# Layer 1's latent attention: two of four probability rows transposed by VectorE and DMA instead of TensorE

## The chip, the core and the metric

The kernel runs on one core of one Trainium2 chip. The core has TensorE for matrix products (PE in the profile, its weight loads PEld), VectorE (DVE), ScalarE (ACT), GpSimd (POOL) and SyncE (SP), which issues most of the DMAs; 16 DMA engines carry them. The metric is the time of one execution on the device in microseconds, given as the median of several runs.

## What is computed

The reference is a four-layer model on 2,048 tokens of width 256 in float32. Each layer adds an attention-like part and a feed-forward part to its input; both read the same layer norm. The change lies in layer 1's attention, a latent attention with 16 heads and 4 sequences of 512 tokens:

```
scores = einsum('bqhd,bkhd->bhqk', qf, kf) * softmax_scale
causal = tril(ones((s, s)))
scores = where(causal, scores, min)
attn   = softmax(scores, axis=-1)
out    = einsum('bhqk,bkhd->bqhd', attn, v)
return out.reshape(b, s, N_HEADS * D_V) @ wo
```

Layer 1's feed-forward part is a product-key lookup (for each token the best 8 of 512 experts, whose rows are gathered from DRAM) and a gated MLP.

## The kernel before

Everything is float32. Streams of work are written as Python generators, and `weave` takes steps from several of them in turn, by costs that each step yields. Layer 1 (`layer1`) weaves four: the latent attention (`latent_pieces`), the product-key lookup (`product_key_pieces`), the rest of the gated MLP (`glu_pieces`), and at the end the routing of layer 2. The scheduler then orders each engine's instructions by its own priorities, except where the kernel pins them (`tc.keep_in_program_order`, or `c.chain`, which ties each pinned instruction to the last pinned one).

The attention works on the latent form: keys of 64 latent and 64 rotary dimensions are shared by all heads (`kf`), values are the 64 latent dimensions (`cv`), and the value and output projections are multiplied together ahead (`wz`, by `carry`). The loop over `s` runs through 64 head-sequences (16 heads times 4 sequences). Two successive `s`, an even and an odd one, are a pair `p` that shares one query projection, one value product and one output projection's half.

For each `s` there are four rows of 128 queries, row `i` having `(i+1)*128` keys (causal):

- `probabilities(s, i)`: a score matmul on PE (L985), an eviction on DVE that adds the mask and finds the row's extreme (L988, writes `pr` and `nm`), an exponential on ACT that also sums (L992), a reciprocal on DVE (L1108) and a scaling by it on ACT (L1110). Buffers `pr0` to `pr3` are double.
- `turned(s-1, j)`: the value product needs the probabilities with the keys on the partitions. PE transposes each 128x128 block (L1117), 10 blocks per `s`, into PSUM tiles `tr`; DVE (for j = 0 and 2) or ACT (for j = 1 and 3) copies them into `PT` (L1121). This is done one `s` behind the scores.
- `queries(p+1)`, in every even `s`: matmuls (L1072 to L1077), an ACT copy to `pes`, four DMAs on SP that swap its quarters into `psw` (L1082), two ACT scalings into `qf`. `rotate`, in the next odd `s`, applies the rotary tables on DVE (L1091 to L1094) and completes `qf`.
- the value product of pair p (L1253): 8 matmuls of 512, 384, 256 and 128 columns, the two heads in the two column halves of the array (64 output columns each), then an ACT copy to `zT` (L1259). After every second pair, the output projection (L1267) and its addition to `x` on DVE (L183).

`product_key_pieces` first ranks experts (8 rounds, each with a DMA `routed<-both` and back on SP, L1359 and L1361), then for each of 16 token tiles loads `tok` by SP (L1369), gathers 8 experts on GpSimd's queue (L1371), multiplies on DVE (L1381) and adds on DVE (L177).

Layer 3's attention (`full_attention`), which the change does not touch, already transposes on DVE and DMA: DVE transposes within 32x32 blocks (L1598, tile `Y`), four DMAs write the strips of 32 partitions to a DRAM buffer (L1603), one DMA on the same queue reads it back in the wanted order (L1607, `PT`), and the value product (L1642) reads `PT` in blocks of 128 columns made of four runs of 32.

Of the kernel before, what the change touches and what calls it, by code (L numbers as in the profile page):

```python
# [16 lines left out]
P = 128  # L17
# [3 lines left out]
TPB = SEQ // P  # L21
# [9 lines left out]
class Ctx:  # L31


    def __init__(self, tc, stack):
        self.tc, self.nc = tc, tc.nc
        self.stack = stack
        self.n = 0
        pool = lambda name, **kw: stack.enter_context(tc.tile_pool(name=name, **kw))
        self.keep = pool("keep", bufs=1)
        self.ln = pool("ln", bufs=1)  # L40
        self.psum = pool("psum", bufs=4, space=bass.MemoryType.PSUM)
        self.users, self.then, self.later, self.pinned = {}, None, [], False
        self.trickle, self.chained = [], None

    def tile(self, pool, shape, tag, dtype=F32, **kw):
        self.n += 1
# [11 lines left out]
    def chain(self, ins):  # L58


        last, self.chained = self.chained, ins.ins
        if last is not None:
            self.tc.add_manual_dep(
                ins.ins, last.name,
                mybir.DependencyInfo(mybir.DependencyClass.NoSync, mybir.DependencyReason.DATA),
                reason="chain",
            )
        return ins
# [942 lines left out]

def latent_pieces(c, a, keep, open_pool):

# [47 lines left out]
    def queries(p):  # L1063

        g, b, pair = p // 8, p // 2 % 4, p % 2
        if p % 8 == 0:
            carry(g)
        wpe0, wpe1, wl0, wl1, _ = weights[g]
        tokens = slice(b * SEQ, (b + 1) * SEQ)
        cols = slice(pair * P, (pair + 1) * P)  # L1070
        pe, pl = c.ps(), c.ps()
        nc.tensor.matmul(pl, lhsT=wl0[:, cols], rhs=qa0[:, tokens], start=True, stop=False)  # L1072
        upper = nc.tensor.matmul(pe, lhsT=wpe1[:, cols], rhs=qa1[:KL, tokens], start=True, stop=False)
        with tc.issue_after(upper.ins), tc.high_priority(offset=200):
            nc.tensor.matmul(pl, lhsT=wl1[KL:, cols], rhs=qa1[KL:, tokens], start=False, stop=True)
        with tc.high_priority(offset=100):
            nc.tensor.matmul(pe, lhsT=wpe0[:, cols], rhs=qa0[:, tokens], start=False, stop=True)  # L1077

        pes, psw = (c.tile(pool, [P, SEQ], n, bufs=1) for n in ("pes", "psw"))
        nc.scalar.copy(pes, pe)  # L1080
        for to in range(0, P, 32):
            nc.sync.dma_start(psw[to : to + 32, :], pes[to ^ 32 : (to ^ 32) + 32, :])  # L1082
        qf = c.tile(pool, [P, 2, SEQ], "qf")
        nc.scalar.mul(qf[:KL, 0, :], pl[:KL, :], -scale)
        nc.scalar.mul(qf[KL:, 1, :], pl[KL:, :], -scale)
        qfs[p] = qf
        return pes, psw, qf

    def rotate(pes, psw, qf):
        pec = c.tile(pool, [P, SEQ], "pec", bufs=1)  # L1090
        nc.vector.tensor_mul(pec, pes, cosq)  # L1091
        tc.keep_in_program_order(nc.vector.tensor_mul(psw, psw, sinq))
        nc.vector.tensor_add(qf[:KL, 1, :], pec[:KL, :], psw[:KL, :])
        nc.vector.tensor_add(qf[KL:, 0, :], pec[KL:, :], psw[KL:, :])  # L1094

    def probabilities(s, i):
        p, h = s // 2, s % 2
        b = p // 2 % 4
        if i == 0:
            totals[s] = c.tile(pool, [P, TPB], "total")  # L1100
        rinv = totals[s]
        prs[s].append(exp_scores(
            c, pool, late, qfs[p][:, h, :], kf[:, h, b * SEQ : (b + 1) * SEQ], i, rinv[:, i : i + 1]
        ))
        if i >= TPB - 2:

            done = slice(0, i + 1) if i < TPB - 1 else slice(i, i + 1)
            nc.vector.reciprocal(rinv[:, done], rinv[:, done])  # L1108
            for j in range(TPB)[done]:
                nc.scalar.mul(prs[s][j], prs[s][j], rinv[:, j : j + 1])  # L1110

    def turned(s, j):

        pt = c.ps("tr")
        n = SEQ - j * P
        for i in range(j, TPB):
            nc.tensor.transpose(  # L1117
                pt[:, (i - j) * P : (i - j + 1) * P], prs[s][i][:, j * P : (j + 1) * P], c.ident
            )
        copy = nc.scalar.copy if j % 2 else nc.vector.tensor_copy  # L1120
        return lambda: copy(PTs[s][:, START[j] : START[j] + n], pt[:, :n])  # L1121

    START = (0, 512, 896, 1152)
    qfs, prs, totals, PTs, zTs = {}, {}, {}, {}, {}
    rope = c.tile(pool, [P, SEQ], "psw", bufs=1)
    nc.scalar.dma_start(rope, a["l_rope"])
# [2 lines left out]
    def latents(b):  # L1129

        if b < 2:
            rooms = [c.tile(pool, [P, 1280], "PT")[:, :1024]]
        elif b == 2:
            rooms = [c.tile(pool, [P, SEQ], "zT", bufs=3) for _ in range(2)]
# [38 lines left out]
    for b in range(NB):  # L1173
        tokens = slice(b * SEQ, (b + 1) * SEQ)
        lats.append(latents(b))
        for t in range(TPB):
            tt = b * TPB + t
            pl = c.ps()[:, : QL + KL]
            project_tokens(c, pl, wa, slice(0, QL + KL), slice(tt * P, (tt + 1) * P))
            lat = lats[b][t]  # L1180
            nc.vector.tensor_copy(lat, pl)
            sq = c.tile(pool, [P, QL + KL], "pr1")
# [12 lines left out]
        rot = c.tile(pool, [P, SEQ], "pr3")  # L1195
        nc.vector.tensor_mul(rot, pk, rope)
        rots.append((rot, tokens))
        yield 1.2
# [16 lines left out]
        finish(b)  # L1215
        yield 1.9

    copy = None
    yield 1.9
    for s in range(65):  # L1220
        if s < 64:
            prs[s] = []
        for i in range(TPB):
            if s < 64:
                probabilities(s, i)
            if s > 0:
                if i == 0:
                    PTs[s - 1] = c.tile(pool, [P, 1280], "PT")
                ready, copy = copy, turned(s - 1, i)
                if ready:  # L1230
                    ready()
            if i == 0 and s % 2 == 1 and s < 63:
                rotate(*turning)
            yield 0.85
            if i == 1 and s % 2 == 0 and s < 62:
                turning = queries(s // 2 + 1)
                yield 2.6
        if copy:
            copy()
            copy = None  # L1240
        if s > 0:
            del prs[s - 1]
        if s % 2 == 1:
            continue
        if s == 0:
            continue

        p = s // 2 - 1
        g, b, pair = p // 8, p // 2 % 4, p % 2
        z = c.ps("acc")  # L1250
        for j in range(TPB):
            for h in range(2):
                tc.keep_in_program_order(nc.tensor.matmul(  # L1253
                    z[h * KL : (h + 1) * KL, j * P :], lhsT=cv[:, b * TPB + j, :],
                    rhs=PTs[s - 2 + h][:, START[j] : START[j] + SEQ - j * P],
                    start=(j == 0), stop=(j == TPB - 1),
                ))
        zTs[pair] = c.tile(pool, [P, SEQ], "zT", bufs=3)
        nc.scalar.mul(zTs[pair], z, kv_w)  # L1259
        yield 2.1  # L1260
        if pair == 1:
            wz = weights[g][4]
            for t in range(0, TPB, 2):
                po = v3(c.ps("acc"), DM)
                for j in range(2):
                    for k in range(2):
                        nc.tensor.matmul(  # L1267
                            po[:, j, :], lhsT=zTs[k][:, (t + j) * P : (t + j + 1) * P],
                            rhs=wz[:, k, :], start=(k == 0), stop=(k == 1),
                        )  # L1270
                add_pair(c, b * TPB + t, po)
                if g == 3 and t == TPB - 2:
                    c.part_done(b)
                yield 1.7


def product_key_pieces(c, a, keep, pool, dram, xn):
# [88 lines left out]
    def gather(t, k):  # L1366
        if k == 0:
            tok[t] = c.tile(pool, [P, DM], "tok", bufs=2)
            nc.sync.dma_start(tok[t], xn[t * P : (t + 1) * P, :])  # L1369
        e = c.tile(pool, [P, 2 * DM], "e", bufs=8)  # L1370
        nc.gpsimd.indirect_dma_start(  # L1371
            out=e, out_offset=None, in_=a["p_experts"],
# [36 lines left out]
def layer1(c, a, xn, following):  # L1409


    with ExitStack() as stack, ExitStack() as right:
# [7 lines left out]
        latent = latent_pieces(c, a, keep, lambda: pool_of("l_h", 2))  # L1420

        def glu_units():
            same = dict(tanh=True, bufs=5)
# [995 lines left out]
```

## Time and profile before

| What | Value |
|---|---|
| Median of 3 runs | 3007.26 us (3001.71 to 3009.33) |
| Profiled execution: own time | 2998.64 us |
| Profiled execution: span, mean granted clock | 2996.9 us, 0.988 |
| Busy: PE, DVE, ACT, POOL | 2892.5, 2136.6, 1391.8, 856.3 us |
| Scores of layer 1's attention, from the first 512-column score matmul to the last | 859 to 1470 us |

A group row reads: line, engine, operation, out<-in by the program's names, shape, count | busy us, mean ns of one | idle time of the engine just before, and what ended it. A float32 matmul is recorded as two passes, so counts of matmuls in the profile are twice the program's (transposes have one). Durations of matmuls overlap: what one costs in a row of many is the distance from one start to the next. "`<- issue`" marks time in which the engine waited for nothing that the profile shows.

### The profile page before, as it was taken

How to read it: one execution, taken by the hardware profiler on the slowest of the kernel's cores; microseconds unless marked ns; L12 is line 12 of the kernel's file. 1: busy time of each engine (PE TensorE's matmuls, PEld its weight loads, DVE VectorE, ACT ScalarE, POOL GpSimd, SP SyncE). 2: the span in 40 equal slices, each digit the busy share in tenths (PEclk: the TensorE clock that was granted, in tenths of full speed). 3: DMA queues.
4: the chain of work that ended last, by engine and by line, in shares of the span. 5: the costliest groups of instructions: out<-in, count | busy, mean ns of one | idle time of the engine just before them, and what ended most of it. 6: DMA issues, size and time to landing. Idle time of an engine off the chain costs nothing.

```text
span 2996.9 us, 40558 instructions
## 1 busy us (share of the span) xinstructions
PE 2892.5 (97%) x13812; PEld 1958.9 (65%) x13812; DVE 2136.6 (71%) x5434; ACT 1391.8 (46%) x3336; POOL 856.3 (29%) x681
## 2 busy tenths in 40 slices
PE   8999999999999999999978899999999999999999
PEld 5566666566755655555656588888888856666666
DVE  5777778787777787868643777777777756666666
ACT  4444445444376666656622454445444333333332
POOL 0565565656310033332023200000000033333331
PEclk9999999999999999999988999999999999999999
DMA  3333333242221145342223434443544300000000
GB/s 133 97 109 116 102 95 110 90 134 73 100 70 37 46 120 123 104 99 82 84 79 116 136 115 123 129 148 119 151 123 148 124 0 22 22 22 22 22 1 29
DMA packets 138366, 268.03 MB, mean 89 GB/s; under 512 B 19664, under 2 KB 99040, under 8 KB 133808
## 3 DMA queue, kind: packets, MB, share of 16 engines
q1 hardware_dynamic: 123696, 217.65, 23.1%
q0 software_dynamic: 14176, 47.01, 6.2%
q8 instruction: 109, 1.79, 0.2%
q14 instruction: 97, 0.79, 0.1%
q10 hardware_dynamic: 288, 0.79, 0.1%
HBM read 202.21 MB, written 54.26 MB: 86 GB/s over the span
## 4 chain that ended last, share of the span: by engine, by line
PE 81%; DVE 8%; ACT 4%; another core or an unknown queue 2%; issue 2%; POOL 1%; DMA 1%; SPq 0%; ACTq 0%; DVEq 0%; POOLq 0%
PE mm L329 16%; PE mm L159 14%; PE mm L985 7%; PE acc L329 6%; PE tr L329 6%; PE acc L1642 5%; PE acc L1001 4%; PE tr L823 3%; PE acc L1253 2%; PE tr L237 2%; PE acc L1267 2%; PE tr L1117 2%; PE acc L801 2%; PE mm L167 2%
## 5 line engine op out<-in xcount | busy, mean ns | idle before, releaser
L992 ACT ACTIVATE pr<-pr,nm 128x128 f32<-128x128 f32 (+3 forms) x512 | 286.1, 559 | 290.6 <-DVE nm L988 272.3
L988 DVE CUSTOM_DVE_ANT_0 pr<-mm,late 128x128 f32<-128x128 f32 (+3 forms) x512 | 245.6, 483 | 124.0 <-PE mm L985 108.1
L159 PE MATMUL mm<-xnT,wu 128*128 128x512 f32 x624 | 287.8, 599 | 0.0
L340 ACT COPY part<-mm 128x512 f32<-128x512 f32 (+1 forms) x372 | 177.7, 478 | 213.3 <-PE mm L329 205.0
L329 PE MATMUL mm<-token_sums,unit_sums 128*128 128x512 f32 (+1 forms) x624 | 267.5, 511 | 2.2 <-ACT part L340 2.2
L1371 POOL DMA_INDIRECT e<-in_p_experts,ids x128 | 130.0, 1016 | 477.1 <-DVE x L177 330.7
L159 PE MATMUL mm<-xnT,w_in 128*128 128x512 f32 x512 | 229.2, 593 | 0.6 <-DVE cy L591 0.6
L491 DVE SCALAR_TENSOR_TENSOR x<-acc,cw,x 128x128 f32<-128x128 f32 x372 | 128.8, 346 | 107.8 <-PE acc L329 106.1
L591 DVE SCALAR_TENSOR_TENSOR cy<-mm,ws,cy 128x509 f32<-128x509 f32 (+2 forms) x216 | 160.2, 744 | 51.1 <-ACT cy L587 47.2
L159 PEld LDWEIGHTS mm<-xnT,wu 128*128 128x128 f32 x624 | 115.4, 192 | 118.7 <-issue 110.9
L985 PE MATMUL mm<-kf,qf 128*128 128x128 f32 (+3 forms) x512 | 173.9, 442 | 3.1 <-DVE qf L1094 2.8
L985 PE MATMUL mm<-k,q 128*128 128x128 f32 (+3 forms) x512 | 172.0, 440 | 4.0 <-DVE nm L988 3.4
L761 POOL TENSOR_TENSOR G<-G,CB 128x1024 f32<-128x1024 f32 x64 | 151.5, 2367 | 81.7 <-DVE G L724 75.6
L744 ACT ACTIVATE xD<-xc,ws 128x128 f32<-128x128 f32 x256 | 83.9, 390 | 193.1 <-POOL y L785 183.6
L329 PEld LDWEIGHTS acc<-down_sums,hidden_sums 128*128 128x128 f32 x744 | 112.1, 192 | 85.1 <-issue 82.9
L159 PEld LDWEIGHTS mm<-xnT,w_in 128*128 128x128 f32 x512 | 96.5, 190 | 104.4 <-issue 94.9
L1642 PEld LDWEIGHTS acc<-PT,V 128*128 128x128 f32 x1280 | 154.5, 193 | 5.4 <-issue 2.0
L273 POOL TENSOR_TENSOR down_sums<-wu 128x256 f32<-128x256 f32 x8 | 5.9, 734 | 520.7 <-PE mm L329 411.9
L1642 PE MATMUL acc<-PT,V 128*128 128x128 f32 x1280 | 154.6, 276 | 0.0
L724 DVE TENSOR_TENSOR_SCAN G<-G,eye 128x1024 f32<-128x1024 f32 x64 | 148.2, 2315 | 0.0
L1117 PEld LDWEIGHTS tr<-con,pr 128*128 128x128 f32 x640 | 80.0, 142 | 92.0 <-issue 22.7
L474 DVE TENSOR_TENSOR whole<-mm,part 128x512 f32<-128x512 f32 x128 | 88.5, 692 | 68.4 <-PE mm L329 68.4
(440 smaller groups left out, 6783.6 us busy)
## 6 DMA issues: line engine op xcount, KB each, us to landing
turned<-Y SPq DMA_DIRECT2D x252, 160.0 KB
PT<-turned SPq DMA_DIRECT2D x63, 640.0 KB
G<-own SPq DMA_DIRECT2D x64, 512.0 KB
w_in<-in_m_units SPq DMA_DIRECT2D x16, 1024.0 KB
eb<-since SPq DMA_DIRECT2D x96, 128.0 KB
wu<-in_o_units SPq DMA_DIRECT2D x6, 1536.0 KB
wo<-in_m_units SPq DMA_DIRECT2D x16, 512.0 KB
psw<-pes SPq DMA_DIRECT2D x128, 64.0 KB
```

Source lines behind the costliest of these rows:

```text
L159: c.nc.tensor.matmul(out, lhsT=w[:, d, cols], rhs=c.xnT[:, d, tokens], start=(d == 0), stop=(d == 1))
L329: self.kept(self.c.nc.tensor.matmul(bank, lhsT=lhsT, rhs=rhs, start=first, stop=True, skip_group_check=not first))
L340: self.c.nc.scalar.copy(r, bank)
L591: nc.vector.scalar_tensor_tensor(y[:, j:], src[:, : SEQ - j], conv[:, k, 3 - j : 4 - j], y[:, j:], ALU.mult, ALU.add,)
L724: tc.keep_in_program_order(nc.vector.tensor_tensor_scan(flat, flat, eye.rearrange("p h t -> p (h t)"), 0.0, ALU.mult, ALU.add))
L761: nc.gpsimd.tensor_mul(G, G, seqs[b][2][:, t, :][:, None, :].to_broadcast([P, HG, P]))
L985: kept(nc.tensor.matmul(sc, lhsT=q[:, i * P : n], rhs=k[:, :n], start=True, stop=True))
L988: nc.vector.tensor_tensor_reduce(out=pr, in0=sc, in1=late[:, SEQ - n :], scale=scale, scalar=-NEG, op0=ALU.add, op1=ALU.min, accum_out=nm,)
L992: nc.scalar.activation(pr, pr, AF.Exp, bias=nm, scale=-1.0, accum_out=total)
L1117: nc.tensor.transpose(pt[:, (i - j) * P : (i - j + 1) * P], prs[s][i][:, j * P : (j + 1) * P], c.ident)
L1371: nc.gpsimd.indirect_dma_start(out=e, out_offset=None, in_=a["p_experts"], in_offset=bass.IndirectOffsetOnAxis(ap=ids[:, t, k : k + 1], ax ...
L1642: kept(nc.tensor.matmul(zs[:, i], lhsT=head["V"][:, j, h, :], rhs=head["PT"][:, :, i * (i + 1) // 2 + j, :], start=(j == 0), stop=(j == i),))
```

## The change

In layer 1's attention, rows 0 and 1 of each `s` (3 of the 10 blocks) are still transposed on PE, now in one PSUM tile with one ACT copy. Rows 2 and 3 (7 blocks) are transposed by DVE within 32x32 blocks into `Y`, written to DRAM by four DMAs on SP and read into `PT` by a fifth on SP, as in layer 3; the last `s` does them on PE. `PT` gets three buffers instead of two, `pr0` to `pr3`, `Y`, `pes` and `psw` have one, `zT` two. The value product becomes 20 matmuls of 128 columns and comes later: for the pair (2p, 2p+1) it stands in `s = 2p+3` after its third score. Score, transposition, query, value and output matmuls are chained in program order on PE, and the swap and strip DMAs in program order on SP (`chain` now keeps one chain per engine). One of the query projection's PSUM tiles moves from `mm` to `tr`. Reciprocals and scalings are done for rows 0 and 1 together and 2 and 3 together. `rotate` works in place. The `tok` loads of the product-key lookup move from SP's queue to GpSimd's. The gated MLP's and the lookup's own work is unchanged.

```diff
     def chain(self, ins):
-        last, self.chained = self.chained, ins.ins
+        last = self.chained.get(ins.ins.engine)
+        self.chained[ins.ins.engine] = ins.ins
...
-        pe, pl = c.ps(), c.ps()
...
+        pe, pl = c.ps(), c.ps("tr")
+        for out, lhsT, rhs, start, stop in (
+            (pl, wl0[:, cols], qa0[:, tokens], True, False),
+            (pe, wpe1[:, cols], qa1[:KL, tokens], True, False),
+            (pl, wl1[KL:, cols], qa1[KL:, tokens], False, True),
+            (pe, wpe0[:, cols], qa0[:, tokens], False, True),
+        ):
+            c.chain(nc.tensor.matmul(out, lhsT=lhsT, rhs=rhs, start=start, stop=stop))
...
-            nc.sync.dma_start(psw[to : to + 32, :], pes[to ^ 32 : (to ^ 32) + 32, :])
+            c.chain(nc.sync.dma_start(psw[to : to + 32, :], pes[to ^ 32 : (to ^ 32) + 32, :]))
...
-            c, pool, late, qfs[p][:, h, :], kf[:, h, b * SEQ : (b + 1) * SEQ], i, rinv[:, i : i + 1]
+            c, pool, late, qfs[p][:, h, :], kf[:, h, b * SEQ : (b + 1) * SEQ], i, rinv[:, i : i + 1],
+            kept=c.chain, bufs=1,
         ))
-        if i >= TPB - 2:
-            done = slice(0, i + 1) if i < TPB - 1 else slice(i, i + 1)
+        if i % 2:
+            done = slice(i - 1, i + 1)
...
-    def turned(s, j):
-        pt = c.ps("tr")
-        n = SEQ - j * P
-        for i in range(j, TPB):
-            nc.tensor.transpose(
-                pt[:, (i - j) * P : (i - j + 1) * P], prs[s][i][:, j * P : (j + 1) * P], c.ident
-            )
-        copy = nc.scalar.copy if j % 2 else nc.vector.tensor_copy
-        return lambda: copy(PTs[s][:, START[j] : START[j] + n], pt[:, :n])
+    def turn_strips(s, i):
+        if i == 2:
+            Ys[s] = c.tile(pool, [P, 896], "Y", bufs=1)
+        nc.vector.transpose(wide(Ys[s], i), strips(prs[s][i]))
+        if i == TPB - 1:
+            room = c.tile(dram, [4, 32, 4, 224], "strips")
+            PTs[s] = c.tile(pool, [P, 1280], "PT", bufs=3)
+            Y = Ys.pop(s)
+            for a in range(4):
+                c.chain(nc.sync.dma_start(
+                    room[:, :, a, :].rearrange("b r e -> r b e"),
+                    Y[a * 32 : (a + 1) * 32].rearrange("p (b e) -> p b e", b=4),
+                ))
+            c.chain(nc.sync.dma_start(PTs[s][:, :896], room.rearrange("b r a e -> (b r) (a e)")))
+
+    def turned(s, rows):
+        if s not in PTs:
+            PTs[s] = c.tile(pool, [P, 1280], "PT", bufs=3)
+        pt, n = c.ps("tr"), 0
+        for i in rows:
+            for j in range(i + 1):
+                c.chain(nc.tensor.transpose(
+                    pt[:, n * P : (n + 1) * P], prs[s][i][:, j * P : (j + 1) * P], c.ident
+                ))
+                n += 1
+        if rows[0] == 0:
+            return lambda: nc.scalar.copy(PTs[s][:, 896:], pt[:, : 3 * P])
+        return lambda: nc.scalar.copy(wide(PTs[s], rows[0]), strips(pt[:, : n * P]))
...
+    def values(p):
+        g, b, pair = p // 8, p // 2 % 4, p % 2
+        z = c.ps("acc")
+        for i in range(TPB):
+            for j in range(i + 1):
+                for h in range(2):
+                    c.chain(nc.tensor.matmul(
+                        z[h * KL : (h + 1) * KL, i * P : (i + 1) * P], lhsT=cv[:, b * TPB + j, :],
+                        rhs=block(2 * p + h, i, j), start=(j == 0), stop=(j == i),
+                    ))
...
-    for s in range(65):
+    for s in range(66):
...
+            if i == 0:
+                if s % 2 == 1 and s < 63:
+                    rotate(*turning)
+                yield from islice(pieces, 1)
+            if i == 1 and s % 2 == 0:
+                yield from islice(pieces, 1)
+                if s < 62:
+                    turning = queries(s // 2 + 1)
+                    yield 2.6
+            if i == 2 and s % 2 == 1 and s > 2:
+                pieces = values(s // 2 - 1)
+                yield 2.6
+            if i == TPB - 1 and s < 63:
+                turn_strips(s, 2)
+                turn_strips(s, 3)
+            if s < 64 and i == TPB - 1:
+                copy = turned(s, (0, 1))
...
-            nc.sync.dma_start(tok[t], xn[t * P : (t + 1) * P, :])
+            nc.gpsimd.dma_start(tok[t], xn[t * P : (t + 1) * P, :])
```

More of the change, by code (lines that the diff above doesn't have):

```diff
@@ L42, in __init__ @@
         self.users, self.then, self.later, self.pinned = {}, None, [], False
-        self.trickle, self.chained = [], None
+        self.trickle, self.chained = [], {}
     def tile(self, pool, shape, tag, dtype=F32, **kw):
@@ L1008, in heads_out, with latent_pieces @@
         yield 1.7
-def latent_pieces(c, a, keep, open_pool):
+def latent_pieces(c, a, keep, open_pool, dram):
     nc, tc = c.nc, c.tc
@@ L1070, in queries @@
         cols = slice(pair * P, (pair + 1) * P)
-        pe, pl = c.ps(), c.ps()
[L1072 to L1077, printed above, removed]
+        pe, pl = c.ps(), c.ps("tr")
[6 more added lines that the diff above has]
+            c.chain(nc.tensor.matmul(out, lhsT=lhsT, rhs=rhs, start=start, stop=stop))
         pes, psw = (c.tile(pool, [P, SEQ], n, bufs=1) for n in ("pes", "psw"))
@@ L1089, in rotate @@
     def rotate(pes, psw, qf):
-        pec = c.tile(pool, [P, SEQ], "pec", bufs=1)
-        nc.vector.tensor_mul(pec, pes, cosq)
+        nc.vector.tensor_mul(pes, pes, cosq)
         tc.keep_in_program_order(nc.vector.tensor_mul(psw, psw, sinq))
-        nc.vector.tensor_add(qf[:KL, 1, :], pec[:KL, :], psw[:KL, :])
-        nc.vector.tensor_add(qf[KL:, 0, :], pec[KL:, :], psw[KL:, :])
+        nc.vector.tensor_add(qf[:KL, 1, :], pes[:KL, :], psw[:KL, :])
+        nc.vector.tensor_add(qf[KL:, 0, :], pes[KL:, :], psw[KL:, :])
     def probabilities(s, i):
@@ L1110, in probabilities, with strips, wide, block @@
                 nc.scalar.mul(prs[s][j], prs[s][j], rinv[:, j : j + 1])
-    def turned(s, j):
-        pt = c.ps("tr")
-        n = SEQ - j * P
-        for i in range(j, TPB):
-            nc.tensor.transpose(
-                pt[:, (i - j) * P : (i - j + 1) * P], prs[s][i][:, j * P : (j + 1) * P], c.ident
-            )
-        copy = nc.scalar.copy if j % 2 else nc.vector.tensor_copy
-        return lambda: copy(PTs[s][:, START[j] : START[j] + n], pt[:, :n])
-    START = (0, 512, 896, 1152)
+    def strips(ap):
+        return ap.rearrange("p (j a s) -> p j a s", a=4, s=32)
+    def wide(tile, i):
+        lo = 0 if i == 2 else 3
+        return tile[:, :896].rearrange("p (a j s) -> p j a s", j=7, s=32)[:, lo : lo + i + 1]
+    def turn_strips(s, i):
[25 more added lines that the diff above has]
+        return lambda: nc.scalar.copy(wide(PTs[s], rows[0]), strips(pt[:, : n * P]))
+    def block(s, i, j):
+        if i < 2:
+            lo = 896 + (i + j) * P
+            return PTs[s][:, lo : lo + P]
+        return wide(PTs[s], i)[:, j]
+    Ys = {}
     qfs, prs, totals, PTs, zTs = {}, {}, {}, {}, {}
@@ L1131, in latents @@
         if b < 2:
-            rooms = [c.tile(pool, [P, 1280], "PT")[:, :1024]]
+            rooms = [c.tile(pool, [P, 1280], "PT", bufs=3)[:, :1024]]
         elif b == 2:
-            rooms = [c.tile(pool, [P, SEQ], "zT", bufs=3) for _ in range(2)]
+            rooms = [c.tile(pool, [P, SEQ], "zT", bufs=2) for _ in range(2)]
         else:
@@ L1181, in latent_pieces @@
             nc.vector.tensor_copy(lat, pl)
-            sq = c.tile(pool, [P, QL + KL], "pr1")
+            sq = c.tile(pool, [P, QL + KL], "pr1", bufs=1)
             nc.scalar.activation(
@@ L1194, in latent_pieces @@
         project(c, pk, wa, slice(256, 384), tokens)
-        rot = c.tile(pool, [P, SEQ], "pr3")
+        rot = c.tile(pool, [P, 896], "Y", bufs=1)[:, :SEQ]
         nc.vector.tensor_mul(rot, pk, rope)
@@ L1216, in latent_pieces, with out_pieces @@
         yield 1.9
-    copy = None
+    def values(p):
[8 more added lines that the diff above has]
+                    ))
+        for h in range(2):
+            del PTs[2 * p + h]
+        zTs[pair] = c.tile(pool, [P, SEQ], "zT", bufs=2)
+        nc.scalar.mul(zTs[pair], z, kv_w)
+        return out_pieces(g, b) if pair == 1 else iter(())
+    def out_pieces(g, b):
+        wz = weights[g][4]
+        for t in range(0, TPB, 2):
+            po = v3(c.ps("acc"), DM)
+            for j in range(2):
+                for k in range(2):
+                    c.chain(nc.tensor.matmul(
+                        po[:, j, :], lhsT=zTs[k][:, (t + j) * P : (t + j + 1) * P],
+                        rhs=wz[:, k, :], start=(k == 0), stop=(k == 1),
+                    ))
+            add_pair(c, b * TPB + t, po)
+            if g == 3 and t == TPB - 2:
+                c.part_done(b)
+            yield 1.7
+    copy, pieces = None, iter(())
     yield 1.9
-    for s in range(65):
+    for s in range(66):
         if s < 64:
@@ L1225, in latent_pieces @@
                 probabilities(s, i)
[L1226 to L1236, printed above, removed]
-                yield 2.6
-        if copy:
-            copy()
-            copy = None
@@ L1241, in latent_pieces @@
-        if s > 0:
-            del prs[s - 1]
[L1243 to L1274, printed above, removed]
+                yield 0.3
@@ new lines, in latent_pieces @@
+            if copy:
+                copy()
+                copy = None
+            if i == 0:
[9 more added lines that the diff above has]
+                pieces = values(s // 2 - 1)
+                yield 2.6
@@ L1277, in product_key_pieces @@
+            if i == TPB - 1 and s < 63:
[3 more added lines that the diff above has]
+                copy = turned(s, (0, 1))
+            if s == 64 and i < 2:
+                copy = turned(63, (i + 2,))
+            yield 0.5
+        if 0 < s < 64:
+            del prs[s - 1]
+    yield from pieces
 def product_key_pieces(c, a, keep, pool, dram, xn):
@@ L1419, in layer1 @@
         keep = pool_of("l_keep", 1)
-        latent = latent_pieces(c, a, keep, lambda: pool_of("l_h", 2))
+        strips = pool_of("l_dram", 2, space=bass.MemoryType.DRAM)
+        latent = latent_pieces(c, a, keep, lambda: pool_of("l_h", 2), strips)
         def glu_units():
```

## The prediction

> **What bounds the kernel now.** I read the page's first section, then engine busy times cut to layer 1's attention (859 to 1470 us) beside layer 3's (1710 to 2380 us), then the chain of waits and the groups by line in the first stretch.
>
> ```profile
> 859.00:1470.00 611.00, 582.99 (x2624) 341.83 (x2623) 477.56 (x1667) 398.58 (x1058) 122.96 (x122) 0.99 0.32 86
> 1710.00:2380.00 670.00, 660.92 (x3519) 554.79 (x3518) 503.88 (x1678) 327.05 (x927) 25.71 (x26) 0.99 0.45 133
> ```
>
> The columns are us, then busy us of PE, PEld, DVE, ACT and POOL, granted clock, DMA share, GB/s. PE is the busiest in both, DVE second at 78%. Busy PE contains drained pipelines, so I count spacings instead: passes of 512 columns in a row start 427 ns apart, smaller ones in proportion, transposes 109 ns apart, and the two heads of L1253 start 7 ns apart, side by side. So counted, the first stretch holds 518 us of streaming in 611 (ratio 1.18), layer 3's 633 in 670 (1.06). Layer 1 therefore loses 93 us to waits; 31 pairs of head-sequences take 19.7 us each.
>
> ```profile
> by line: PE mm L985 12.0%; PE mm L159 9.6%; PE acc L1253 9.4%; PE acc L1267 7.7%; PE tr L1117 7.7%; PE acc L237 6.1%; DVE pr L988 4.4%; ACT pr L992 3.9%; ACT pr L1110 3.6%; issue 3.4%; PE mm L1073 2.7%; DVE PT L1121 2.3%; PE mm L1072 2.3%;
> ...
> L1117 PE MATMUL tr<-con,pr 128*128 128x128 f32 x610 | 112.2, 282 | 17.8 <-ACT PT L1121 7.5 <-DVE PT L1121 7.0 <-ACT pr L1110 2.1
> ...
> L1117 PEld LDWEIGHTS tr<-con,pr 128*128 128x128 f32 x610 | 76.6, 142 | 88.2 <-issue 21.8 <-ACT PT L1121 20.6 <-DVE PT L1121 16.9
> ```
>
> The transposes hold 7.7% of the chain, 47 us, and wait for copies out of PSUM and scalings: their mean spacing in 900 to 1400 us is 146 ns where 109 would do.
>
> **The change, part by part.** All sums are against the profiled execution, 2998.6 us (span 2996.9), 8.6 us below the median of 3007.3; I carry the difference over to the median.
>
> *Transposes removed.* 63 head-sequences lose 7 of 10: 441 x 0.109 = 48 us of PE. Their waits, 441 x 0.037 = 16 us, go too; what is late next is taken below.
>
> *Value product in 20 matmuls.* Same columns, 2,560 per pair. Layer 3's product already reads strips so:
>
> ```profile
> 1107.46 2.59 PE L1253 MATMUL acc<-PT,cv 128*64 128x512 f32 x16
> ...
> 1999.93 1.75 SPq L1603 DMA_DIRECT2D turned<-Y  x4
> ...
> 2003.34 2.39 PE L1642 MATMUL acc<-PT,V 128*128 128x128 f32 x20
> ...
> 2004.02 0.34 SPq L1607 DMA_DIRECT2D PT<-turned  x1
> ...
> 2008.54 0.58 DVE L1598 STREAM_TRANSPOSE Y<-pr 128x384 f32<-128x384 f32 x1
> ...
> 2010.07 0.70 DVE L1598 STREAM_TRANSPOSE Y<-pr 128x512 f32<-128x512 f32 x1
> ```
>
> Its passes start 112 ns apart, against 107 for 128 columns streamed. In the changed order the heads alternate, so 20 x 0.112 = 2.24 us replaces 2.13: 32 x 0.1 = +3 us. If the heads no longer overlapped it would be +2.2 x 32 = +70; the quads of 128 columns at L1253's end, 109 ns per two passes, are the nearest row and speak against it. [...]
>
> *DVE.* Gone: copies of 512 and 256 columns (0.62 + 0.34 us by spacing). New: the two transposes above, 0.51 + 0.63 by spacing. +0.18 x 63 = +11 us on DVE, 478 to 489, beside other work. [...]
>
> *ACT.* One copy of 384 columns in place of 384 and 128: -0.22 x 64 = -14 us, off the path (399 of 611 busy). Reciprocals and scalings are as many as before. Single `pr` buffers: row 2's next eviction waits for eviction, exponential, reciprocal, two scalings and a transpose, about 5 us of a 9.9 us head-sequence; 0 taken, 1 us of lag would cost 64.
>
> *Loads and queues.* 16 `tok` loads leave SP, where waits for DVE ahead of them came to 98 us; they would have stood before the strips. On POOL each costs about the 1.0 us of a gather (L1371) and stands ahead of eight gathers; POOL is 20% busy: 0 taken, at most 16. On SP each head-sequence adds four writes of 112 KB (0.44 us each to issue), a wait until they land, and one read of 448 KB. Queued behind that wait: the four swap DMAs of the next query, then `rotate`'s products on DVE; also, in eight head-sequences, the lookup's `routed`, and a few weight loads that stand between write and read. By the changed order `rotate` has 6.5 to 8 us of DVE work between a strip transpose and itself, and its swap lands about 8.5 us after: 0 to 1.5 us per pair, 0 to 46 in all; 0 taken, since in light pairs it lies beside the next item.
>
> *The new wait.* The value product waits on PE for the read of the younger head, and every later score is chained behind it. Layer 3's strips: first write issued to read issued 4.1 us (median of 63), read to its last packet 3.5 us, for 640 KB. At 70% of the bytes: 3.0 + 0.5 + 2.8 = 6.3 us. Before it, from the end of that head's fourth score: eviction 0.68, exponential 0.90, reciprocal 0.16, scalings 0.60 + 0.71, transpose 0.70, with hand-overs and DVE's queue about 6; after it, contention (DMA goes from 86 to some 180 GB/s). Together 12.7 us; ends 10.5 and 16. What covers it, summed along the changed PE order from that score to the first matmul that needs the strips: 10.8 us in the 15 pairs without an output projection, 14.2 or more in nearly all others; the MLP's products stand inside in both. So 15 x 1.9 = 29 us of new waiting. In these light pairs PE streams 13.1 us and DVE has 15.7 on the mean, so DVE's limit lies in the same 29, not on top.
>
> Sum: -48 - 16 + 3 + 29 = -32 us. 3007.3 - 32 = **2975 us**.
>
> **Rivals.**
> 1. *Slower: the strips come too late for PE.* With a chain of c us the waiting is 15 (c - 10.8) + 16 (c - 14.2 where positive). It eats the whole 61 at c = 14.5 and decides from there; c = 15.3 gives 85, so +24 (3031), c = 16 gives 107, +46 (3053). For it: the DMAs share engines with the gathers, weight loads of 1.5 MB can stand before a read, and every pair depends on the queue's longest wait. Against: layer 3 lives with 7.6 us of DMA at ratio 1.06, and PE's own delays lengthen the cover.
> 2. *DVE becomes the bound.* Standing each pair's PE streaming beside its DVE work and adding the larger gives 531 us before and 518 after; at the same excess of 1.15 that is -16 (2991), and 0 if `rotate` waits. For it: 489 of DVE against 473 of PE. Against: layer 3 holds 75% DVE with PE nearly full.
> 3. *The chained order also mends the other waits.* 473 us of streaming at a ratio of 1.16 is 549, -62 (2945). For it: layer 3's 1.06. Against: DVE's density there is lower than here afterwards.
> 4. *The heads stop overlapping:* +70 - 32 = +38 (3045). That pairing is unlikely to break, as the order alternates the heads.
>
> **How the numbers follow.** The forecast case has 0.42, with its own range 2955 to 2990; rival 1 0.25, rival 2 0.17 (0.10 of it within the bound, 0.07 faster), rival 3 0.13, rival 4 0.03. About 0.3%, 9 us, is what a measurement of this kernel can tell from no change. Faster by more: 0.42 + 0.13 + 0.07 = 0.62; within: 0.10; slower by more: 0.25 + 0.03 = 0.28. The range reaches down to rival 3 and past its point to 2940, and up into rival 1 to c = 15.3, about 3031: 2940 to 3030 leaves out some 0.05 below and 0.13 above.
>
> **What would show it.** Right: 199 transposes in place of 640, at under 130 ns spacing; score stretch near 580 us; waits for `PT`'s DMA at the value product (L1264) of 20 to 40 us, in light pairs; value passes 112 ns apart in side-by-side pairs; DVE near 84% busy; layers 0, 2, 3 the same. Wrong: waits for `PT` above 60 us, or DVE waiting long for the swap (rival 1); DVE over 88% with PE waiting for its evictions (rival 2); value passes of 64 columns one after the other (rival 4); or a score stretch under 560 us (rival 3).

## The result, and the profile after

The changed kernel took 3141.4 us (median), the kernel before 3008.1 us beside it: ratio 1.0441 (95% interval 1.0417 to 1.0465). It is 4.4% slower; forecast were 2975 us and at most 3030. A second measurement (e5 below) gave 1.0463 (1.0435 to 1.0491).

The first lines to look at are those that answer to the two shown of before: layer 1's attention and layer 3's in the changed kernel, with the same columns (us; busy us of PE, PEld, DVE, ACT, POOL; granted clock; DMA share; GB/s).

```profile
860.00:1625.00 765.00, 606.24 (x3016) 378.50 (x3015) 514.56 (x1721) 408.60 (x1033) 127.31 (x136) 0.89 0.55 146
1850.00:2540.00 690.00, 679.91 (x3612) 566.89 (x3610) 522.42 (x1742) 334.22 (x945) 25.57 (x27) 1.00 0.45 133
```

Layer 3 is as before (TensorE busy in 680 of 690 us). Layer 1's stretch went from 611 to 765 us; in it no engine is full any more: PE 79%, DVE 67%, ACT 53%. So no engine became the bound. The granted clock fell from 0.99 to 0.89. Next, the chain of waits cut to this stretch:

```profile
by line: PE mm L986 9.3%; issue 8.6%; PE acc L1281 7.7%; DMA PT<-strips 6.0%; PE mm L160 5.2%; PE acc L1264 5.0%; PE mm L1079 4.4%; ACT pr L993 3.6%; DVE pr L989 3.5%; PE acc L238 3.5%; DMA strips<-Y 2.9%; ACT pr L1111 2.8%; DVE Y L1128 2.8
```

The transposes, 7.7% before, are gone from the head of the list, and the strips' two DMAs stand there with 8.9%. The waits of the same stretch name who waits for what (us in total, times, longest):

```profile
PE mm L986 <- DVE qf L1095: 66.8, 20, 8.1
...
PE acc L1264 <- DMA PT<-strips: 61.4, 13, 12.1
...
DVE pr L989 <- PE mm L986: 56.7, 43, 10.9
...
DVE pes L1092 <- DMA psw<-pes: 29.7, 8, 8.3
```

The value product (L1264) waits for the strips, as forecast but for twice as long; the scores (L986) wait as long again for the rotation (L1095), which I had taken at nothing. The timeline of one pair shows both, one behind the other:

```profile
1295.47 1.17 DVE L1128 STREAM_TRANSPOSE Y<-pr 128x384 f32<-128x384 f32 x2
...
1296.66 1.74 SPq L1134 DMA_DIRECT2D strips<-Y  x4
...
1297.48 0.59 ACT L1082 COPY pes<-mm 128x512 f32<-128x512 f32 x1
...
1299.39 1.09 PE L1264 MATMUL acc<-PT,cv 128*64 128x128 f32 x14
...
1302.51 0.34 SPq L1138 DMA_DIRECT2D PT<-strips  x1
1302.89 2.43 SPq L1084 DMA_DIRECT2D psw<-pes  x4
...
1306.94 3.25 PE L1264 MATMUL acc<-PT,cv 128*64 128x128 f32 x26 [6.45 <-DMA PT<-strips]
...
1310.12 1.31 PE L986 MATMUL mm<-kf,qf 128*128 128x512 f32 x2
...
1310.29 0.69 DVE L1092 TENSOR_TENSOR pes<-pes,tab 128x512 f32<-128x512 f32 x1 [4.99 <-DMA psw<-pes]
...
1312.32 0.69 DVE L1095 TENSOR_TENSOR qf<-pes,psw 64x512 f32<-64x512 f32 x1
1313.04 0.69 DVE L989 CUSTOM_DVE_ANT_0 pr<-mm,late 128x512 f32<-128x512 f32 x1
...
1313.06 0.49 PE L986 MATMUL mm<-kf,qf 128*128 128x128 f32 x2 [1.31 <-DVE qf L1095]
```

The strips are written from 1296.7 and SyncE issues their read only at 1302.5, 5.8 us later. The swap's source `pes` was ready at 1298.1, but its four DMAs stand behind that read and go out at 1302.9. TensorE has done the 14 value passes that need no strip of the younger head, then stands 6.45 us. VectorE stands 4.99 us in front of the rotation. The next score ends at 1311.4, but its eviction (L989) starts only at 1313.0, when the rotation is done; and TensorE, too, waits for the rotation.

To add this up I set each TensorE instruction's distance to the next against its columns at full rate (427 ns for 512): a distance near twice that (1.8 to 2.2 times) is half speed, the rest is a gap.

| TensorE in layer 1's stretch, us | before | after | difference |
|---|---|---|---|
| streaming at full rate | 522 | 489 | -33 |
| added by half speed | 14 | 47 | +33 |
| gaps ahead of transposes | 29 | 9 | -19 |
| gaps ahead of the value product | 4 | 79 | +75 |
| gaps ahead of scores | 7 | 88 | +82 |
| other gaps | 35 | 52 | +17 |
| window | 611 | 765 | +154 |

Taken by itself, the streaming of the transposes fell from 65 to 20 us, close to the forecast gain of 48; other work that stands in the longer stretch makes it 33 net. The waits ate the gain of 33 and 19 us four times over.

### The profile page after: what moved, and what is told of

The parts are those of the page before. It is cut to its first block, busy times and chain, and to the rows that moved or that the text cites. A ratio compares the mean times of both kernels' runs of the same rounds, so it can differ in the third digit from the quotient of the medians.

```text
span 3141.4 us, 41858 instructions
## 1 busy us (share of the span) xinstructions
PE 2903.6 (92%) x14139; PEld 1988.6 (63%) x14139; DVE 2158.4 (69%) x5432; ACT 1391.1 (44%) x3274; POOL 862.0 (27%) x697
## 4 chain that ended last, share of the span: by engine, by line
PE 76%; DVE 10%; DMA 4%; issue 3%; ACT 3%; another core or an unknown queue 2%; POOL 1%; SPq 1%; DVEq 0%; ACTq 0%; POOLq 0%
PE mm L330 15%; PE mm L160 13%; PE mm L986 6%; PE acc L330 6%; PE tr L330 5%; PE acc L1693 4%; PE acc L1002 3%; PE tr L824 3%; PE acc L1281 2%; PE tr L238 2%; PE acc L802 2%; DMA PT<-strips 1%; PE mm L168 1%; PE mm L2093 1%
## 5 line engine op out<-in xcount | busy, mean ns | idle before, releaser
L989 DVE CUSTOM_DVE_ANT_0 pr<-mm,late 128x128 f32<-128x128 f32 (+3 forms) x512 | 245.1, 485 | 170.1 <-PE mm L986 144.4
L986 PE MATMUL mm<-kf,qf 128*128 128x128 f32 (+3 forms) x512 | 183.4, 474 | 71.3 <-DVE qf L1095 67.4
L986 PE MATMUL mm<-k,q 128*128 128x128 f32 (+3 forms) x512 | 171.8, 440 | 4.0 <-DVE nm L989 3.4
L1264 PE MATMUL acc<-PT,cv 128*64 128x128 f32 x1280 | 101.2, 305 | 67.8 <-DMA PT<-strips 61.4
L986 PEld LDWEIGHTS mm<-kf,qf 128*128 128x128 f32 x512 | 88.7, 205 | 113.6 <-DVE qf L1095 62.1
```

Source lines behind the costliest of these rows:

```text
L986: kept(nc.tensor.matmul(sc, lhsT=q[:, i * P : n], rhs=k[:, :n], start=True, stop=True))
L989: nc.vector.tensor_tensor_reduce(out=pr, in0=sc, in1=late[:, SEQ - n :], scale=scale, scalar=-NEG, op0=ALU.add, op1=ALU.min, accum_out=nm,)
```

## The experiments

My first theory (A): the strips' lateness is the loss, by the value product's wait, the swap queued behind them, and the half speed after such pauses. Its rivals were B (VectorE reaches the rotation late whatever the swap does) and C (the other parts of the change); after four runs D and E name parts of C (single buffers, strict order), and F and G ask whether several waits stand side by side or a constant is left.

Runs e1 to e4 and e9 to e12 were on chips where the kernel before took 2939 to 2940 us, the others on chips where it took 3008 to 3014; so only ratios to the kernel before on the same chip are compared. The changed kernel itself was timed on the second kind only.

**e1: no strips.** TensorE turns all rows, everything else of the change stays.

```diff
-                turn_strips(s, 2)
-                turn_strips(s, 3)
-            if s == 64 and i < 2:
-                copy = turned(63, (i + 2,))
+            if 0 < s < 65 and i < 2:
+                copy = turned(s - 1, (i + 2,))
```

> TensorE turns rows three and four again (640 transposes), strips and their DMAs are gone; the chained order, single pr buffers, 20 value matmuls and GpSimd's token loads stay. Theory A (the strips' lateness is the loss: value product waits 75 us, scores wait 78 us for a rotation whose swap stands behind the strips' wait on SyncE, 33 us of half-speed TensorE after such pauses): 3141 - 75 - 78 - 33 + 48 + 16 = about 3020, within 3000 to 3040. Theory C (the loss is in the other parts: chained order, single buffers, token loads): 3090 or more.

Measured: ratio 1.0431 (1.0405 to 1.0456). With the suspected cause wholly taken out, the loss stayed. Theory A falls as the only cause. In the waits of e1's stretch the place is taken by the transposes, which wait for ScalarE's scalings:

```profile
PE tr L1147 <- ACT pr L1111: 96.6, 54, 4.2
```

**e2: the swap on another queue.**

```diff
-            c.chain(nc.sync.dma_start(psw[to : to + 32, :], pes[to ^ 32 : (to ^ 32) + 32, :]))
+            nc.scalar.dma_start(psw[to : to + 32, :], pes[to ^ 32 : (to ^ 32) + 32, :])
```

> The four swap DMAs of each query are issued from ScalarE's queue in place of SyncE's, nothing else changes. Theory A: the scores' waits for the rotation fall from 78 us to under 30, and the clock wins some 10 us: about 3085, within 3060 to 3105. Theory B (the rotation is late because VectorE gets to it late, whatever the swap does): within 10 us of 3141, the wait for the products of the rotation as long as before.

Measured: 1.0423 (1.0401 to 1.0445). The scores' wait for the rotation went, as A said (67 us to 0.6), and the time did not follow: in e2's waits the strips and the scalings have grown instead.

```profile
PE acc L1264 <- DMA PT<-strips: 81.1, 19, 12.2
...
PE tr L1147 <- ACT pr L1111: 30.0, 18, 6.0
```

**e3: nobody reads the strips.**

```diff
-        return wide(PTs[s], i)[:, j]
+        return wide(kf[:, 0, :], i)[:, j]
```

> The value product reads rows three and four from the keys kf in place of the strips (so these rows' part of the product is left out); the transposes on VectorE, the writes and the read go on as before. Theory A with the two waits side by side: the value product's 75 us go, and 20 of the half-speed time: about 3050. Theory A with one wait behind the other (the rotation's wait, already running, takes over the place of the value product's): 3110 or more. In both the waits for PT's DMA are zero.

Measured: 1.042 (1.0398 to 1.0442). This kernel leaves out the part of the value product that rows three and four make. The mirror image of e2: the value product's wait is zero, and the scores' wait for the rotation is longer than ever:

```profile
PE mm L986 <- DVE qf L1095: 116.0, 22, 12.6
```

**e4: the value product later.**

```diff
-            if i == 2 and s % 2 == 1 and s > 2:
-                pieces = values(s // 2 - 1)
+            if i == 2 and s % 2 == 0 and s > 2:
+                pieces = values(s // 2 - 2)
...
-            PTs[s] = c.tile(pool, [P, 1280], "PT", bufs=3)
+            PTs[s] = c.tile(pool, [P, 1280], "PT", bufs=4)
```

> The value product of each pair moves one head-sequence later (four PT buffers in place of three; wl0, wl1 single, the gated MLP's hT four in place of five, prod in hit's buffer to make room). Theory A: the cover of the strips grows by about 10 us to over 20, so the value product's waits fall from 75 us to under 15; scores' waits for the rotation stay; about 3060, within 3030 to 3090. Theory C: 3110 or more.

Measured: 1.047 (1.0448 to 1.0493). The value product no longer waits (5 us of gaps in all); scores wait 66.5 us for the rotation and transposes 61.4 us for scalings. Four kernels (e1 to e4) with one wait removed, four ratios within half a per cent: whichever wait was taken out, another had grown in its place.

**e5: the changed kernel again**, beside e6 to e8.

> The changed kernel as it is, beside the next three on the same chip, since kernel before took 2939 us there in place of 3008. All theories: 1.044 of the time before, as first measured; the span of the scores 773 us less what the chip gives.

Measured: 1.0463 (1.0435 to 1.0491).

**e6: double buffers for the probabilities.**

```diff
-            kept=c.chain, bufs=1,
+            kept=c.chain,
```

> The changed kernel with two buffers for each row of probabilities (pr0 to pr3) in place of one, as the kernel before had; room from wl0, wl1 single, hT four in place of five, prod in hit's buffer; nothing else. Theory D (the loss is a loop through the single pr buffers: eviction, exponential, reciprocal, scalings, transpose, next eviction): the ratio falls from 1.044 to about 1.00, the score stretch by 100 us or more. Theory E (the strict order written for TensorE is the loss): within 0.01 of 1.044.

Measured: 1.0401 (1.0378 to 1.0424). Theory D (a loop through the single buffers) falls: about 0.6% (e5 less e6) hangs on them.

**e7: TensorE's order free.**

```diff
-            c.chain(nc.tensor.matmul(out, lhsT=lhsT, rhs=rhs, start=start, stop=stop))
+            nc.tensor.matmul(out, lhsT=lhsT, rhs=rhs, start=start, stop=stop)
```

The same is done for scores, transposes and output projection; the value product keeps its own order by `keep_in_program_order`, as before.

> The changed kernel without the written order of TensorE in layer 1's attention (queries, scores, transposes, output projection are placed by the scheduler, the value product's matmuls keep their own order); SyncE's order, single buffers, strips and loads stay. Theory E: the ratio falls to about 1.00 and below. Theory D: within 0.01 of 1.044.

Measured: 1.0446 (1.0411 to 1.0481). Theory E, too, falls as the only cause while the strips stay. TensorE's waits for the strips and for the rotation did shrink, from 61.4 and 66.8 us:

```profile
PE mm L986 <- DVE qf L1095: 26.9, 15, 5.7
...
PE acc L1264 <- DMA PT<-strips: 23.8, 9, 6.9
```

But the free order has a price of its own. The query projection has two products of 64 rows (L1079). In the changed kernel their passes start side by side, as in the kernel before, which gives these matmuls priorities:

```profile
1294.14 0.69 PE L1079 MATMUL mm<-qa,wu 64*128 64x512 f32 x1
...
1294.15 0.69 PE L1079 MATMUL tr<-qa,wl 64*128 64x512 f32 x1
```

The edit takes the chain away and does not bring the priorities back; in e7 the eight passes of a query mostly run one after the other, 4.1 us in place of 3.1:

```profile
1213.97 2.18 PE L1079 MATMUL mm<-qa,wu 64*128 64x512 f32 x4
1215.98 2.07 PE L1079 MATMUL tr<-qa,wl 128*128 128x512 f32 x4
```

Of 64 such pairs of passes, 64 start within 60 ns of each other in the changed kernel and 2 in e7: about 25 us more streaming on TensorE. The same holds, less, for the other kernels with free order: 12 pairs in e14 (some 20 us), 26 in e12, e15 and e16 (15 us), 32 in e11 (13 us), 20 in e17. How much of this reaches the time was not tested.

**e8: the kernel before with token loads on GpSimd's queue.**

```diff
-            nc.sync.dma_start(tok[t], xn[t * P : (t + 1) * P, :])
+            nc.gpsimd.dma_start(tok[t], xn[t * P : (t + 1) * P, :])
```

> The kernel before with the 16 token loads on GpSimd's queue in place of SyncE's, nothing else. My sum: 0 to 16 us (ratio 1.000 to 1.005). If the loads on GpSimd's queue are the loss: 1.02 or more.

Measured: 0.9982 (0.9964 to 1.0000). The loads cost nothing.

**e9: e2 and e4 together** (both diffs above).

> Two edits at once: the value product one head-sequence later (as in e4_late, with its trims) and the swaps on ScalarE's queue (as in e2_swap_act). Each alone left the ratio at 1.047 and 1.042. Theory F (three waits of about the same length stand side by side, each able to hold a pair at about 23 us: strips to value product, swap to rotation to scores, scalings to the transposes of rows one and two; taking one away leaves the others): more than the sum of the two, ratio 1.02 to 1.03, waits of the value product and of the scores under 30 us together, the transposes' wait for scalings still 50 us or more. Theory G (the loss is nothing of these waits but a constant of the new form): 1.035 or more.

Measured: 1.0446 (1.0417 to 1.0475). I had expected 1.02 to 1.03. By that number alone it is theory G's case (1.035 or more); e10 and e11 speak against G. The two waits are gone from the list as forecast, and the third has grown to 90.6 us:

```profile
PE tr L1147 <- ACT pr L1111: 90.6, 28, 8.2
```

**e10: e9, and the transposes of rows one and two two scores later.**

```diff
-            if s < 64 and i == TPB - 1:
-                copy = turned(s, (0, 1))
+            if 0 < s < 65 and i == (1 if s < 64 else 2):
+                copy = turned(s - 1, (0, 1))
```

> As e9, and the transposes of rows one and two stand two scores later in TensorE's order (after the next head's second score; pr0 and pr1 double, the gated MLP's sg single for room). Theory F: with all three waits eased the ratio is 1.00 or below, the transposes' wait under 20 us, score stretch 640 us or less. Theory G: 1.035 or more.

Measured: 1.0233 (1.0204 to 1.0261). With the third wait eased as well the time moves at last, by 2% against e9 on the same chip; not to 1.00 as Theory F wanted. This kernel also has two buffers for `pr0` and `pr1`, which the diff does not show; in e6 two buffers for all four rows were worth about 0.6%. What is left: VectorE waits 50 us for the swap (L1092), scores 28 us for the rotation and 30 us for evictions.

**e11: e9 with TensorE's order free** (e7's diff).

> As e9, and TensorE's order in layer 1's attention left to the scheduler (as in e7). Theory F: the scheduler puts other work ahead of what waits, so 0.99 to 1.02, below e9. If the scheduler's order is no better: like e9. Theory G: 1.035 or more.

Measured: 1.0205 (1.0174 to 1.0236), 2.3% below e9. Freed order, worth nothing while the strips' waits stood (e7), is worth this much once they are eased.

**e12: e1 with the order free and two buffers for each row of probabilities.**

> As e1 (TensorE turns every row, no strips, no strip DMAs), and TensorE's order left to the scheduler, and two buffers for each row of probabilities: what is left of the change is the value product in 20 matmuls, transposes by rows, reciprocals in pairs, the query sum in a tr bank, GpSimd's loads. Theory F: these cost little once the order and the buffers leave room, ratio 1.00 to 1.015. Theory G with the constant in these parts: 1.035 or more, as e1's 1.043.

Measured: 1.0094 (1.0065 to 1.0123). The rest of the change costs about 1% without strips and strict order.

**e13: e10 with the rotation two scores later.**

```diff
             if i == 0:
-                if s % 2 == 1 and s < 63:
-                    rotate(*turning)
                 yield from islice(pieces, 1)
+            if i == 2 and s % 2 == 1 and s < 63:
+                rotate(*turning)
```

> As e10, and the rotation stands two scores later (after the odd head's third score in place of its first). If VectorE's wait for the swap in its queue holds the rest: its 50 us fall under 15, ratio 1.005 to 1.015 from 1.023. If the scores then wait longer for the rotation instead: 1.02 or more.

Measured: 1.0258 (1.0232 to 1.0284), no gain over e10: VectorE still waits 46 us for the swap, and the scores 49 us for the rotation.

**e14: e13 with TensorE's order free.**

> As e13, with TensorE's order left to the scheduler (as e11): all known waits eased while the strips stay. Theory F: 0.985 to 1.005, the only one with a chance to beat the kernel before. If contention of the strips' DMAs or VectorE's work holds it: 1.01 or more.

Measured: 1.0167 (1.0142 to 1.0193), the quickest kernel here with live strips, and slower than before. VectorE's wait for the swap is down to 18 us, yet the granted clock in its stretch is 0.91 and TensorE's gaps are twice those of before (149 us in 685). Some 20 us more go to the query products that no longer stand side by side (see e7).

**e15: e12 with the rotation's first product in its own tile.**

```diff
-        nc.vector.tensor_mul(pes, pes, cosq)
+        pec = c.tile(pool, [P, SEQ], "pec", bufs=1)
+        nc.vector.tensor_mul(pec, pes, cosq)
```

> As e12, with the rotation's first product in its own tile pec, as the kernel before had it (the gated MLP's sg single for room). If the product in place is what was left: ratio 0.995 to 1.003 from 1.009, VectorE's wait for the swap under 12 us. If not: 1.007 or more.

Measured: 1.0053 (1.0038 to 1.0067). The product in place is worth at most the 0.4% between e12 and this; the two ran on different chips, so I leave its size open.

**e16: e1 with the order free, nothing else.**

> As e1 (TensorE turns every row), with TensorE's order left to the scheduler, buffers still single. If the strict order made e1's 1.043: 1.005 to 1.02. If the single buffers did: 1.03 or more, and TensorE still waits over 60 us for scalings.

Measured: 1.0060 (1.0039 to 1.0082). Without strips the strict order alone makes the difference between 1.043 and 1.006; the single buffers do not. Of the 0.6% that is left, up to 0.5% may be the query products described under e7. The same wait as in e1, and the stretch of e1 and of e16 below each other:

```profile
PE tr L1147 <- ACT pr L1111: 10.7, 13, 1.8
```

```profile
860.00:1590.00 730.00, 625.70 (x3445) 404.58 (x3443) 446.96 (x1575) 470.43 (x1151) 127.50 (x136) 0.93 0.30 73
```

```profile
860.00:1505.00 645.00, 621.33 (x3447) 388.56 (x3446) 440.51 (x1577) 455.36 (x1150) 129.47 (x136) 1.00 0.32 83
```

The counts of instructions are equal to a few: the same work, 85 us apart, although e1 ran on the quicker chip.

**e17: strips that nobody waits for.** e16, and beside it strips made, written and read into a dead tile.

```diff
+            if i == TPB - 1 and s < 63:
+                turn_strips(s, 2)
+                turn_strips(s, 3)
-            c.chain(nc.sync.dma_start(PTs[s][:, :896], room.rearrange(...)))
+            if rooms:
+                c.chain(nc.sync.dma_start(dead, rooms[0].rearrange(...)))
+            rooms[:] = [room]
```

> As e16 (TensorE turns every row, order left to the scheduler), and beside it the strips of rows three and four are made by VectorE, written and read back by the same DMAs into a tile that nobody reads, each read taking the strips of the head before, so that no queue waits for a landing (wl0, wl1 single, hT four, prod in hit's buffer for room). The strips' work and traffic without anybody's wait. If the strips cost by being waited for: 1.006 to 1.02. If by traffic or VectorE's 72 us of added transposes: 1.03 or more, as e7's 1.045.

Measured: 1.0329 (1.0297 to 1.0360), 2.7% over e16. So the strips cost even when nobody waits for them. Their trims of buffers are in e12 as well, which is at 1.009. The stretch (all columns as above) is 69% VectorE, so it is not full:

```profile
860.00:1609.00 749.00, 676.30 (x3459) 412.42 (x3458) 514.82 (x1724) 460.28 (x1153) 128.77 (x136) 0.93 0.56 149
```

DMA traffic hardly delays the swap: its last packet ends 2.7 us after its last issue, against 2.1 in e16 (means of 32). But the rotation begins 12.1 us after `pes` against 6.5, although the swap has landed 6.3 us after `pes`: VectorE comes to it late, and the scores wait 23.0 us for it (0.5 in e16). I read this as VectorE's queue, where the transposes stand ahead of evictions, reciprocals and rotation; that queue was not varied by itself.

**e18: the strict order alone in the kernel before.** Queries, scores, transposes, value product and output projection are chained as written.

```diff
-            nc.tensor.transpose(
+            c.chain(nc.tensor.transpose(
```

> The kernel before with the strict order alone: queries, scores, transposes, value product and output projection are chained on TensorE as they are written; double buffers, transposes by columns, eight value matmuls, SyncE's token loads stay. If the strict order is enough by itself: 1.02 to 1.05, with TensorE waiting for scalings and copies at the transposes (L1117's place) over 50 us. If it costs only with the single buffers or rows as they stand in e1: 0.995 to 1.01.

Measured: 1.0360 (1.0327 to 1.0392). This written order is enough by itself. The query matmuls also lose the priorities of the kernel before, but still start side by side (62 of 64 pairs). That any strict order costs as much is not shown: e10, strict with the transposes elsewhere, is 2% quicker than e9. In e18's waits the transposes (L1120 here) wait for the scalings:

```profile
PE tr L1120 <- ACT pr L1113: 51.2, 67, 2.6
```

The main finding is a table of two by two (ratio to the kernel before):

| | TensorE's order free | strict order |
|---|---|---|
| TensorE turns all rows | 1.006 (e16) | 1.043 (e1) |
| strips by VectorE and DMA | 1.045 (e7) | 1.044 and 1.046 (the change, e5) |

Each of the two alone brings nearly the whole loss, and the two together cost little more than one. That is why no single undoing helped. Two reservations: e1 ran on the quicker chip, the others on the slower ones; and the left column holds the query products' lost pairing, up to 0.8% in e7 and 0.5% in e16 if all of it reached the time, which would leave the finding as it is.

## Why the prediction was wrong, point by point

*Transposes removed, -48 and -16.* Right. Their streaming in the stretch fell by 45 us (65 to 20), and their waits by 19. Net streaming fell by 33, since the stretch after holds slightly more other work.

*Value product, +3.* Right. The heads alternate 5 to 7 ns apart, pairs of passes about 109 ns; a product that is not interrupted takes 2.13 us from its first to its last start. Rival 4 did not happen.

*Token loads, 0.* Right (e8). *Single buffers, 0.* Nearly right: about 0.6% (e6 beside e5), and no gain from e16 to e12, which ran on different chips.

*The new wait, +29.* The mechanism was right, the size was not: 75 us more of gaps. The chain from the fourth score's eviction to the landed strips, put at 12.7 us, took 15.9 on the mean, 10.4 to 23.5. VectorE's and ScalarE's part was right (6.4 against about 6). Wrong was the scaling by bytes: I took 70% of layer 3's times, since the strips have 70% of its bytes. From first write to read it took 5.6 us, not 3.0, and from the read to its last packet 3.9, not 2.8. Layer 3's 4.1 us for more bytes, beside 5.4 here for fewer (medians of 63 from first write to read), shows that bytes alone did not set the time; no run here separates a part that does not shrink with them, and what made the strips slower here than there was not isolated. With 15.9 in rival 1's own formula, 15 x 5.1 + 16 x 1.7 = 104 us, the rival would have stood at about 3050: the right side, and still 90 us short. Its signs came true: waits for `PT` above 60 us (61.4), and VectorE waiting for the swap (29.7 us).

*The rotation, 0 of 0 to 46.* Wrong: 82 us more of gaps ahead of scores, most of them waits for the rotation (66.8 us). I counted VectorE's work ahead of it as cover; but the swap left SyncE 2.5 us after `pes` on the mean (longest 9.6, behind the strips' wait; before, 0.03 on the mean), and VectorE reached the rotation 11.4 us after `pes`.

*VectorE's transposes "beside other work".* Wrong in kind. I asked whether VectorE would be full; it never was (67%). Yet e17 shows 2.7% lost to strips that nobody waited for. As I read it, a half-idle engine delays whatever stands behind its new instructions; e17 has the strips' DMA traffic too, so this is not shown apart from it.

*The strict order.* With the waits of the strips and the rotation this is the step that failed: either alone brings nearly the whole loss (e7; e1 and e18), and this one had no term in the sum. I named it only as what "every later score is chained behind", and in rival 3 as a possible gain. In the kernel before it costs 3.6% by itself (e18), with TensorE waiting 51.2 us at the transposes for the scalings of ScalarE, an engine that the forecast had put off the path. The forecast summed waits as if each removed wait freed its own time; but with this fixed order on TensorE several waits of nearly the same length stand side by side. e2, e3, e4 and e9 show it: each wait that was removed came back as another.

*The clock.* Not in the sum at all: 33 us. The same 40 passes of a value product stand in the timelines of e1 and of the changed kernel, there in 2.40 us at a granted clock of 1.00, here in 4.54 at 0.50:

```profile
1160.48 2.40 PE L1264 MATMUL acc<-PT,cv 128*64 128x128 f32 x40
```

```profile
1227.46 4.54 PE L1264 MATMUL acc<-PT,cv 128*64 128x128 f32 x40
```

Half speed began in or within 4 us after 27 of the 32 pauses over 2 us in this stretch, as the last section shows.

*Still open.* Why even e14 stays 1.7% slower (some 50 us, of which the query products may be 20), and how e17's 2.7% divides between VectorE's queue and the traffic. A kernel with strips in which VectorE's order is changed by itself was not run. No version of the changed kernel beat the kernel before.

## What to carry to other kernels

Before you price a removed wait, list every other wait that ends soon after it: in a pipeline as tightly coupled as this one the gain was only the distance to the next one (e1 to e4: four ratios within half a per cent), and a strict order on one engine can turn lateness elsewhere into its own idle time (e18: 51.2 us at the transposes). Two changes that each look like the culprit may both be sufficient, so undo them together as well as one by one; a two-by-two table of runs shows it. And "beside other work" need not be cover: where an engine takes its instructions one after the other, as VectorE did when an eviction stood 1.6 us behind the rotation in the timeline above, ask what stands behind the new instruction, not only whether the engine is full. When you free an order, look for pairs that the order had kept together.

## What the runs showed of the hardware that was not expected

In the changed kernel TensorE fell to half speed after short pauses: one whole value product then took 4.1 us from first to last start in place of 2.1. In this trace the record of the granted clock holds 1.0 and 0.5 alone, and every spell at 0.5 in layer 1's stretch lasts 3.4 us or a multiple of it, as do the spells at 1.0. Such a spell began in the pause or within 4 us after it for 15 of 15 pauses over 3.4 us, for 12 of 17 pauses of 2 to 3.4 us, and for 9 of 41 of 0.5 to 2 us; the last is no more than chance would give, with 29 spells in 765 us. Most pauses of 2 to 3.4 us were thus already followed by it; from what length on a pause brings it was not shown beyond these counts. By them, waits of over 2 us were often worth more than their length here: 33 us more of half speed came on top of some 150 us of added gaps.

A swap issued from ScalarE's queue occupied that queue for 2.5 us per four DMAs (as it did SyncE's, 2.4; medians of 32), most often in front of an exponential of ScalarE; e2, e9 to e11, e13 and e14 carry this cost.
